# A recurrent kernel's opening: how its first inputs are read and turned

## The chip, the cores and the metric

The kernel runs on one core of one Trainium2 chip. The metric is the device time of one execution in microseconds (us); lower is better. The engines are called as the profile calls them: PE (TensorE, matrix products), DVE (VectorE), ACT (ScalarE), POOL (GpSimd) and SP (SyncE, which here only starts DMA transfers). Each engine works through its own instructions in program order and waits on semaphores for the others.

## What is computed

A gated recurrent unit over 128 steps for a batch of 64, with input and state 512 wide; every fourth step the state is sent through one more layer. The output is the input plus the states.

```python
def step(h, inp):
    x_t, prop = inp
    comb = jnp.concatenate([x_t, h], axis=-1)
    z = jax.nn.sigmoid(comb @ Wz + bz)
    r = jax.nn.sigmoid(comb @ Wr + br)
    comb2 = jnp.concatenate([x_t, r * h], axis=-1)
    h_cand = jnp.tanh(comb2 @ Wh + bh)
    h_new = (1.0 - z) * h + z * h_cand
    h_next = jnp.where(prop, jnp.tanh(h_new @ Wp + bp), h_new)
    return (h_next, h_new)
_, ys = jax.lax.scan(step, h0, (xs, do_prop))
return jnp.transpose(ys, (1, 0, 2))
...
x = x + _L0_cond_ref(x, cond_1024, ...)
```

x is 64 x 128 x 512 (batch, step, width), h0 64 x 512, the three gate matrices 1024 x 512 (the upper half, called wx in the kernel, meets x; the lower half, wh, meets h), Wp 512 x 512, all float32.

## The kernel before

The batch is split in two halves of 32 (h) and the width in four quarters of 128 (q); a step of x or h lies in on-chip memory as 128 partitions (quarter, batch row) by 2 x 128. For a product the state or the input must stand turned, width on the partitions. h is turned by DVE's transpose (L963); x by the same instruction at L547, in `join(t)`, which writes `xT`.

The part of the gates that comes from x doesn't depend on the state. It is made for groups of four steps at a time and kept in `cp`. For steps 0 to 3, `plain(t)` makes it with ordinary products of `xT` and `wx` (L392 is the line of the helper that emits every matmul), and DVE adds the biases on the way out of PSUM (L759). From group 1 (steps 4 to 7) on, `batch` makes it with a two-level fast scheme (Strassen's): seven products of seven, for which sums of pieces of `wx` (`tt`, `tf`, `tw`, L592, most on POOL, some on DVE, once at the start) and sums of pieces of `xT` (`s12r`, `o12`, `o34`, ..., L624 to L661, on POOL, in every group) must stand ready. The results are folded together by POOL (L848) and placed into `cp` by ACT and by DMA. From step 2 on the recurrent products use a one-level scheme of the same kind (`gates_seven`).

All operations are first collected in a plan: each has an engine, what it reads and writes, and a cost. The order in which they are then emitted comes from a table, `ORDER`, a compressed list of positions, found by a search beforehand; it fixes the order on each engine. PE's products of x fill the time in which the recurrence waits for other engines.

In the opening (L481 to L535) the transfers are these. SP starts two quarters of x of step 0, then wx: rows 0 and 1 of the gates R and Z in four pieces of 256 KB (`load_wx(..., True)`), the rest of R, Z and H in sixteen pieces of 128 KB, one per quarter of the partitions and pair of rows; then wh of R, Z and H, Wp, its bias, and later steps of x. ACT starts the other two quarters of step 0, the four of step 1 and three bias rows. POOL starts x of steps 2 and 3 (eight pieces), h0 (four) and x of steps 4 to 7 (eight). Two one-element copies on POOL, `held` (L456), stand ahead of these: the first waits until step 0 of x has landed, the second, ahead of x 4 to 7, until the last quarter of the Z weights has. Steps 0 to 7 of x stay in `xj`, where the output is later formed in place.

PE begins with 42 idle products of zeros (L900). The rows of x are read in pieces of 512 bytes (one quarter of one batch row).

Of the kernel before, what the change touches and what calls it, by code (L numbers as in the profile page):

```python
# [13 lines left out]
ALU = mybir.AluOpType  # L14
# [146 lines left out]
c-n2-2VhoNoha~oZtuO9@B0#x5E#lhGdj*VIyy}qM@L<Ku5aAkQFql{x4G`FK6Tv?S}3805_$<G0Rn^`I)oZ}C!qugW#|wXAhh>CH(?z2z5C;T%Kw~u^W`h|  # L161
o|}XXi1^@78$v()^oCIK3-tZ}u@T?<-e^R?_HE)X{(``Je}}Lviy(}5KKQ_Z?TrsV{P2Gfo!i@Q3xe><*My(`MBra~>B}#DzHk1sp&mV6e%2(u`qf^&-X@5*
;9uV7KKJ?jmkVEd>7|$7eDke$--X6Ezxkc_zw*X6UwZf5Z@l~NTf~>sUEX-*3s7ddbg9kj(xs4a;DE_zk{(HQo<+>eo0$iX$;7q$qGi6cI&W;A^ZfG#y?gg|
9mjE<L3!BFylw>1)i3HkJ<o&rg)ctJJ<1gp7UtXk{c#TK;^p_sCtMf4l6^VXA-J9U2$+|09sYS>-aqH%`R25|>p9Cx<ny_o|2&RuyE!K}<(hJF9EV|K1=fLF
hyAINyp~)`?re_G3BvO%{1vw6zIiCOEjK=IOYRxpPrp}-c<Zfq-d>p-o3}F84`O9*EySjrq9~#$YMP0R#ks{fRaJ>sKmW?-YIE3%Ts07H<U~=a%3+E!JI77W
O^5WH90~%QLmW3bH!U}@Q;&%`W<rkRxbZo1T+VVBTi1u@M(6DK1!QP_bAxhasS%yEK~X(=49xY-mFETkT6xYb&2{Jpf%9^4Nv<S^o@V>xo@PsPUG3tcBElAL
WyQPM{G!4a^Yd?IF-^Ocy_Th~W-;8v^@Z$}PoT@$%h{}w%Mm0K!jpPBdm?)(J1Xx~wnK<ovOxgvw}@!VPRWJGvd6N`kl&X*+Ua=q9Ar*++ME6Eq3oe-6!Ckq
!MBfQljOa|EXFrxzp*uowq<vuwt?-bZ7H4?d465?ZQFL%W}jJ;HBG`@optN8^;y<55ls>rT9K9IW!WX!8i+bjpIr(iZZFR+gQ!crydb*(rp(VGeI6W!Ig%Bs
v#MH^eWp4)FsIJV5;L+hvIJ4|-1O}9?5ymR>~kzDNrF%bQ;NoB$7ZKyi7DCfFfa$c+3{J4;U!6$l^vIz219tlsO%U}2?SaYIIdf_ZbP%fvwgEeQr4*Kz!W_w
%Muht<rl&BD5GiZnfA<+%)QLx)bQ+s4E8wFA6li^Tn^q__h7;RI7lWhuQc19d6>DAxev10?5)hLOdE7Rh65;>jG`14Mg^BLmon&b23Hq5UCM+PGZ+3$p)7al  # L170
# [1145 lines left out]
```

## Time and profile before

| | |
|---|---|
| median of three runs | 1226.2 us (1226.2, 1226.74, 1223.36) |
| the profiled execution | 1223.71 us |
| its span, first to last instruction | 1221.9 us |
| mean granted clock of PE | 0.998 |
| PE busy from 0 to 2 us, and from 60 to 80 us | 0.80 us, 19.85 us |
| HBM read, written | 24.84 MB, 16.78 MB |

The span is what the profile shows; the execution's own time is 1.8 us more. A row of a timeline gives the start, the time, the engine, the line, the operation, what it writes and reads, how many such instructions are merged, and in brackets the idle time of the engine before it with what ended it. A busy time is a share of one stretch: PE's is near full in almost all of them.

### The profile page before, as it was taken

To read this page: it belongs to the slowest core of one execution; us is meant where nothing else is said; L and a number is where in the kernel's file an instruction comes from. 1 tells how busy PE (TensorE), PEld (TensorE's weight loads), DVE (VectorE), ACT (ScalarE), POOL (GpSimd) and SP (SyncE) were. 2 spreads that over 40 slices of the span, in tenths; PEclk is the share of its full clock that TensorE was granted. 3 is DMA by queue.
4 is the path that set the end of the run, shared out by engine and by line. 5 is a ranking of instruction groups with operands and counts; after the bars stand their busy time and mean duration, and the time that the engine had idled before them with its cause. 6 is when DMAs were issued, how large, how long until landed. Compare 5 with 4: busy or idle time off the path is not lost.

```text
span 1221.9 us, 85156 instructions
## 1 busy us (share of the span) xinstructions
PE 1203.6 (99%) x37418; PEld 1151.8 (94%) x37418; DVE 866.6 (71%) x2833; ACT 778.6 (64%) x2309; POOL 960.1 (79%) x1510
## 2 busy tenths in 40 slices
PE   8799999999999999999999999999999999999997
PEld 5689999999999999999999999999999999999997
DVE  3967776677777777777776767777676777767775
ACT  1366666666666666666666666666666666666663
POOL 7998778787877887787887878876888878778852
PEclk9999999999999999999999999999999999999999
DMA  8212122122221222122212222211222212221122
GB/s 227 68 44 58 50 68 58 50 53 53 58 57 52 58 54 53 44 53 59 55 45 59 53 57 61 53 49 51 56 58 53 51 47 59 56 59 46 43 54 58
DMA packets 92018, 71.48 MB, mean 58 GB/s; under 512 B 7484, under 2 KB 87484, under 8 KB 91647
## 3 DMA queue, kind: packets, MB, share of 16 engines
q1 hardware_dynamic: 90328, 64.84, 20.5%
q8 instruction: 294, 4.82, 1.6%
q0 software_dynamic: 640, 0.92, 0.3%
q14 instruction: 78, 0.63, 0.2%
q10 hardware_dynamic: 678, 0.27, 0.1%
HBM read 24.84 MB, written 16.78 MB: 34 GB/s over the span
## 4 chain that ended last, share of the span: by engine, by line
PE 94%; POOL 3%; DMA 1%; issue 0%; DVE 0%; ACT 0%; SPq 0%; ACTq 0%; POOLq 0%; DVEq 0%
PE ps_e L392 16%; PE ps_r L392 15%; PE ps_b L392 13%; PE ps_y L392 12%; PE ps_x L392 12%; PE ps_q L392 11%; PE ps_z L392 9%; PE ps_a L392 6%; POOL tt L592 2%; DMA wx<-in_L_cond_Wh_dram 0%; DMA wx<-in_L_cond_Wz_dram 0%; DMA wh<-in_L_cond_Wr_dram 0%; POOL tf L592 0%; DMA xj<-in_x_dram 0%; POOL tw L592 0%
## 5 line engine op out<-in xcount | busy, mean ns | idle before, releaser
L392 PE MATMUL ps_z<-wh,sa 128*32 128x128 f32 x3904 | 168.7, 273 | 0.4 <-issue 0.4
L1058 POOL TENSOR_TENSOR sa<-hT 128x64 f32<-128x64 f32 x244 | 77.1, 322 | 111.6 <-DVE hT L963 80.1
L848 POOL TENSOR_TENSOR st<-mb,mb 128x768 f32<-128x768 f32 x77 | 141.1, 1833 | 10.1 <-ACT cp L872 4.3
L392 PE MATMUL ps_r<-wh,rhT 128*32 128x128 f32 x4096 | 144.8, 273 | 0.7 <-DVE rhT L963 0.7
L392 PE MATMUL ps_e<-wh,rhT 128*32 128x128 f32 x4096 | 144.5, 273 | 0.1
L963 DVE STREAM_TRANSPOSE hT<-h 128x128 f32<-128x128 f32 x318 | 97.4, 309 | 54.8 <-ACT h L1010 42.6
L392 PEld LDWEIGHTS ps_z<-wh,sa 128*32 128x32 f32 x3904 | 131.9, 110 | 3.5 <-issue 1.0
L848 POOL TENSOR_TENSOR mb<-mb,mb 128x768 f32<-128x768 f32 x62 | 113.8, 1835 | 19.7 <-ACT mb L815 14.3
L392 PEld LDWEIGHTS ps_r<-wh,rhT 128*32 128x32 f32 x4096 | 125.5, 110 | 3.1 <-DVE rhT L963 1.3
L1152 POOL TENSOR_TENSOR xj<-xj,h 128x256 f32<-128x256 f32 x127 | 93.2, 735 | 44.7 <-DVE h L1135 44.3
L872 ACT COPY cp<-st 64x384 f32<-64x384 f32 x248 | 125.0, 508 | 5.2 <-POOL st L848 1.0
L392 PEld LDWEIGHTS ps_e<-wh,rhT 128*32 128x32 f32 x4096 | 124.6, 110 | 1.9 <-DVE rhT L963 0.4
L1066 DVE TENSOR_TENSOR ps_z<-ps_z,keep 128x128 f32<-128x128 f32 x244 | 72.2, 296 | 41.9 <-PE ps_z L392 33.1
L1006 ACT COPY ps_r<-cp 128x128 f32<-128x128 f32 x256 | 69.2, 270 | 47.1 <-DVE h L1135 29.1
L392 PE MATMUL ps_y<-tw,s 128*32 128x192 f32 x1488 | 98.1, 328 | 0.1
L848 POOL TENSOR_TENSOR st<-mb 128x768 f32<-128x768 f32 x47 | 86.2, 1834 | 12.2 <-ACT cp L872 5.0
L392 PE MATMUL ps_e<-wh,hT 128*32 128x128 f32 x2144 | 90.6, 273 | 1.5 <-ACT ps_e L1006 0.7
L547 DVE STREAM_TRANSPOSE xT<-xj 128x256 f32<-128x256 f32 x128 | 82.6, 657 | 10.8 <-DMA xj<-in_x_dram 10.7
L1058 POOL TENSOR_TENSOR sa<-hT,sa 128x64 f32<-128x64 f32 x244 | 78.5, 322 | 12.5
L392 PE MATMUL ps_r<-wt,hT 128*32 128x128 f32 x1952 | 84.9, 273 | 0.0
L392 PE MATMUL ps_b<-wh,hT 128*32 128x128 f32 x1952 | 84.4, 273 | 0.0
L392 PE MATMUL ps_b<-wt,sa 128*32 128x128 f32 x1952 | 84.3, 273 | 0.0
(179 smaller groups left out, 3617.8 us busy)
## 6 DMA issues: line engine op xcount, KB each, us to landing
cp<-st SPq DMA_DIRECT2D x248, 96.0 KB
out_dram<-xj SPq DMA_DIRECT2D x254, 64.0 KB
xj<-in_x_dram SPq DMA_DIRECT2D x240, 64.0 KB
wx<-in_L_cond_Wh_dram SPq DMA_DIRECT2D x8, 128.0 KB
wh<-in_L_cond_Wr_dram SPq DMA_DIRECT2D x8, 128.0 KB
wh<-in_L_cond_Wz_dram SPq DMA_DIRECT2D x8, 128.0 KB
wh<-in_L_cond_Wh_dram SPq DMA_DIRECT2D x8, 128.0 KB
wp<-in_L_cond_Wp_dram SPq DMA_DIRECT2D x8, 128.0 KB
```

What stands on the lines that cost most here:

```text
L392: nc.tensor.matmul(dst, lhsT=lhsT, rhs=rhs, start=start, stop=True, skip_group_check=True)
L547: lambda: nc.vector.transpose(out=xT_(g)[:, i].rearrange("p c (a h b) -> p h (c a) b", a=S, h=S), in_=xj(t).rearrange("p h (e k) -> p h k ...
L592: fn = {"+": lambda: eng.tensor_add(dst, a, b), "-": lambda: eng.tensor_sub(dst, a, b)}[op]
L848: el("pool", 768, lambda: nc.gpsimd.tensor_add(dst, a, b), reads, writes, rank=FOLD)
L872: el("act", 384, lambda h=h, own=own: nc.scalar.copy(cp_(2 * g + a)[own, nb, h].rearrange("p b g u -> p (b g u)"), st_(n)[own, h].rearrang ...
L963: add("dve", 0.23, lambda: nc.vector.transpose(out=dst, in_=src), reads, writes, land=0.08, main=True)
L1006: el("act", n, lambda: nc.scalar.copy(dst, src), reads, writes, "+" + bank, main=True)
L1058: tensor(lambda: nc.gpsimd.tensor_sub(sa[:, n], a, b), reads, [("sa", t, n)], n=64, engine="pool")
L1066: tensor(lambda: nc.vector.tensor_add(dst, a, b), reads, writes, used_)
L1152: el("pool", 256, lambda: nc.gpsimd.tensor_add(x_out, x_out, h_(new_)), [("h", new_, 0), ("h", new_, 1)] + xk_, xk_)
```

## The change

Steps 0 to 3 of x are read as whole rows: one transfer of 64 rows of 2 KB per step (`load_flat`) into memory that the fast scheme uses only later (`spare`, two of the three `mb` buffers). They are turned by PE: `turn_x` multiplies a piece of the rows with a 64 x 64 unit matrix (`square`, made by POOL with a memset and an affine_select), 16 products per step, into the PSUM banks q and y, and DVE copies the result to `xT`. SP starts step 0, ACT steps 1 to 3.

All of wx is loaded in twelve pieces of 256 KB (gate and row), R and Z first, H last. h0 and x of steps 4 to 7 are started by SP instead of POOL, h0 behind wx, x 4 to 7 behind wh of R; x of steps 0 to 3 is loaded a second time, in the layout that the output needs, behind all of wh. The `held` copies are gone. 16 idle products stand where 42 stood. The order table is replaced as a whole (its encoded text is left out here).

A switch `ONE` is added by which products of group 1 could skip the inner level of the fast scheme (`flat=`, `rows_of`, `one`, `twos`); it is empty, so none does, and its hunks are left out.

```diff
@@ -317,6 +335,8 @@
     U2 = J // 2
     U4 = J // 4
     R, Z, H_ = range(3)
+    IDLES = 16
+    ONE = ()
     assert V * NQ == P and D == H and J == P and T % 8 == 0
 
     RINGS = {
@@ -351,13 +371,15 @@
     bias_row = wt.rearrange("p a k n -> p (a k n)")[0:1, : 3 * H].rearrange("p (i n) -> p i n", i=3)
     ones = wt.rearrange("p a k n -> p (a k n)")[0:1, 3 * H : 3 * H + V]
     dummy = new("dummy", [1, 1])
-    held = new("held", [P, 2])
+    square = wt.rearrange("p a k n -> p (a k n)")[0:B, 3 * H + B : 3 * H + 2 * B]
 
     steps_in = new("xj", [P, RINGS["xj"], S, J])
     xT_ = ring("xT", [P, Q4, C, P])
     cp_ = ring("cp", [P, C, S, 2, 3, U2])
     mb_ = ring("mb", [P, 2, 2, S, 3, U2])
     st_ = ring("st", [P, S, 2, 3, U2])
+    spare = [mb_(n).rearrange("p m b h g u -> p (m b h g u)")[:B] for n in (-1, -2)]
+    flat = lambda t: spare[t // 3][:, t % 3 * H : (t % 3 + 1) * H]
     xj = lambda t: steps_in[:, t % RINGS["xj"]]
     bias_x = steps_in[:, -2:].rearrange("p t h j -> p (t h j)")[:, : 3 * J].rearrange("p (c i u) -> p c i u", c=C, i=3)
     c5_ = ring("c5", [P, 2, S, 3 * U4])
@@ -418,13 +440,8 @@
     def queue(engine):
         return {"sp": nc.sync, "actq": nc.scalar, "poolq": nc.gpsimd}[engine]
 
-    def load_step(t, q, engine):
-        load(
-            engine,
-            lambda: queue(engine).dma_start(
-                out=xj(t)[part(q)], in_=x[:, t, ts(q, J)].rearrange("(h b) j -> b h j", h=S)),
-            [("xj", t, h, q) for h in range(S)], size=32.0, cost=0.4,
-        )
+    def load_flat(t, engine):
+        load(engine, lambda: queue(engine).dma_start(out=flat(t), in_=x[:, t, :]), [("xn", t)], size=128.0)
 
     def rows(ap, t, h):
         return ap[ts(h, V), t, :].rearrange("b (q j) -> q b j", q=NQ)
@@ -436,25 +453,9 @@
             if t < 3 * Q4:
                 plan.behind.append((late, op.index))
 
-    def load_wx(i, k, wide=False):
-
+    def load_wx(i, k):
         w = gates_in[i][:D].rearrange("(p k) n -> p k n", k=K)
-        if wide:
-            load("sp", lambda: nc.sync.dma_start(out=wx[:, k, i, :], in_=w[:, k]),
-                 [("wx", 0, i, k)], size=256.0, cost=0.43)
-            return
-        for q in range(NQ):
-            load(
-                "sp",
-                lambda q=q: nc.sync.dma_start(out=wx[part(q), k : k + 2, i, :], in_=w[part(q), k : k + 2]),
-                [("wx", 0, i, k + n, q) for n in range(2)], size=128.0, cost=0.43,
-            )
-        for n in range(2):
-            plan.whole(("wx", 0, i, k + n), [("wx", 0, i, k + n, q) for q in range(NQ)])
-
-    def hold(n, src, reads):
-        op = add("pool", 0.1, lambda: nc.gpsimd.tensor_copy(held[P - V : P, n : n + 1], src), reads, [("held", n)])
-        heads.setdefault("poolq", []).append(op.index)
+        load("sp", lambda: nc.sync.dma_start(out=wx[:, k, i, :], in_=w[:, k]), [("wx", 0, i, k)], size=256.0, cost=0.43)
 
     def load_wh(dst, w, keys, over=(), ks=K):
 
@@ -479,49 +480,56 @@
         )
 
     add("dve", 0.3, lambda: nc.vector.memset(zeros, 0.0), (), [("zeros", 0)])
+    add("pool", 0.16, lambda: nc.gpsimd.memset(square, 0.0), (), [("square", 0)])
+    add("pool", 0.25, lambda: nc.gpsimd.affine_select(
+        out=square, in_=square, compare_op=ALU.not_equal, fill=1.0, base=0,
+        pattern=[[-1, B]], channel_multiplier=1), [("square", 0)], [("square", 0)])
     add("pool", 0.2, lambda: nc.gpsimd.memset(ones, 1.0), (), [("ones", 0)])
-    for q in range(NQ):
-        load_step(0, q, ("sp", "actq")[q % 2])
-    load_wx(R, 0, True)
-    for q in range(NQ):
-        load_step(1, q, "actq")
-    for i, k in ((Z, 0), (R, 1), (Z, 1)):
-        load_wx(i, k, True)
+    begin = len(plan.ops)
+    load_flat(0, "sp")
+    load_flat(1, "actq")
+    load_wx(R, 0)
+    load_flat(2, "actq")
+    load_wx(Z, 0)
+    load_flat(3, "actq")
+    load_wx(R, 1)
+    load_wx(Z, 1)
     for i in range(3):
         load_bias(i)
-    opening = list(range(2, len(plan.ops)))
+    opening = list(range(begin, len(plan.ops)))
     plan.behind += list(zip(opening, opening[1:]))
-    for i, k in ((R, 2), (Z, 2), (H_, 0), (H_, 2)):
+    for i, k in ((R, 2), (Z, 2), (R, 3), (Z, 3), (H_, 0), (H_, 1), (H_, 2), (H_, 3)):
         load_wx(i, k)
     add(
         "act", 1.5, lambda: nc.scalar.activation(dummy, ones[:, 0:1], AF.Sigmoid),
         [("ones", 0)], [("dummy", 0), ("row_free", 0)],
     )
-    hold(0, xj(0)[P - V : P, 0, 0:1], [("xj", 0, 0, 3)])
-    for t in (2, 3):
-        for q in range(NQ):
-            load_step(t, q, "poolq")
     for q in range(NQ):
         load(
-            "poolq",
-            lambda q=q: nc.gpsimd.dma_start(
+            "sp",
+            lambda q=q: nc.sync.dma_start(
                 out=h_(0)[part(q)], in_=h0[:, ts(q, J)].rearrange("(h b) j -> b h j", h=S)
             ),
             [("h", 0, h, q) for h in range(S)], size=32.0,
         )
     for h in range(S):
         plan.whole(("h", 0, h), [("h", 0, h, q) for q in range(NQ)])
-    hold(1, wx[P - V : P, 3, Z, 0:1], [("wx", 0, Z, 3, 3)])
-    for h in range(S):
-        for q in range(NQ):
-            load(
-                "poolq",
-                lambda h=h, q=q: nc.gpsimd.dma_start(
-                    out=steps_in[part(q), Q4 : 2 * Q4, h, :], in_=x[ts(h, V), Q4 : 2 * Q4, ts(q, J)]),
-                [("xj", t, h, q) for t in range(Q4, 2 * Q4)], size=64.0,
-            )
-    for i in range(3):
+
+    def load_four(g):
+        for h in range(S):
+            for q in range(NQ):
+                load(
+                    "sp",
+                    lambda h=h, q=q: nc.sync.dma_start(
+                        out=steps_in[part(q), g * Q4 : (g + 1) * Q4, h, :], in_=x[ts(h, V), g * Q4 : (g + 1) * Q4, ts(q, J)]),
+                    [("xj", t, h, q) for t in range(g * Q4, (g + 1) * Q4)], size=64.0,
+                )
+
+    load_wh(wh[0], gates_in[0][D:], ("wh", 0, 0))
+    load_four(1)
+    for i in (1, 2):
         load_wh(wh[i], gates_in[i][D:], ("wh", 0, i))
+    load_four(0)
     load_wh(wp, Wp, ("wp", 0))
     for q in range(NQ):
         load("sp", lambda q=q: nc.sync.dma_start(
@@ -552,7 +560,7 @@
             [("xT", g, i)], land=0.08,
         )
         turns.append(turned.index)
-        if 0 < t < 2 * Q4:
+        if Q4 < t < 2 * Q4:
             plan.behind.append(tuple(turns[-2:]))
 
     def outer(kb, nb, ka):
...
@@ -901,9 +932,29 @@
                 bank.rearrange("p a n -> p (a n)")[part(i % NQ)], lhsT=zeros[:, :V], rhs=zeros,
                 start=True, stop=True), reads, writes or [("bits", 0)], rank=1e6)
 
-    idle(42)
+    idle(IDLES)
+    turn_keys = [take("q"), take("y")]
+
+    def turn_x(t):
+        bank = "qy"[t % 2]
+        ps = scratch[bank].rearrange("p a n -> p (a n)")[:, t // 2 * C * P : (t // 2 + 1) * C * P]
+
+        def unit():
+            for k in range(K):
+                for q in range(NQ):
+                    mm(ps[part(q), ts(k, B)], flat(t)[:, q * P + k : (q + 1) * P : K], square, True)
+
+        n = -1 - t // 3
+        own = [("turned", t)]
+        first = [turn_keys[t % 2]]
+        old = [("mb", n, m, b, a) for m in range(2) for b in range(2) for a in range(2)]
+        add("pe", 0.46, unit, [("xn", t), ("square", 0)] + ([] if t < 2 else first),
+            own + (first if t < 2 else []) + old + [("row_free", 0)], "+" + bank)
+        el("dve", 256, lambda: nc.vector.tensor_copy(xT_(0)[:, t].rearrange("p c n -> p (c n)"), ps),
+           own + first, [("xT", 0, t)], bank)
+
     for t in range(Q4):
-        join(t)
+        turn_x(t)
     spread_key = take("y")
     spread_ps = scratch["y"][:, 0:3]
 
```

More of the change, by code (lines that the diff above doesn't have):

```diff
@@ L796, in blocks, with one @@
             return [("mb", n, m, b, a) for m in range(2)]
+        def one(bank, m, left, right, reads, first):
+            def unit():
+                for h in range(S):
+                    for c in range(2):
+                        mm(ps[bank][part(2 * h + c), m].rearrange("p d (g u) -> p d g u", g=3),
+                           left[:, ts(h, V)], right[:, c::2], first)
+            add("pe", 0.327, unit, reads + ([] if first else [key[bank]]), [key[bank]], "+" + bank)
         def product(bank, j, start):
@@ L802, in product @@
                 right, rk = factor(i, j)
[L804 to L810 removed]
+                one(bank, m, left, right, lk + rk, first)
                 plan.due += long / count
```

318 lines of the change are left out of this document (175 added, 143 removed).

## The prediction

> **What bounds the kernel now.** The page first: one engine, TensorE, fills the span.
>
> ```profile
> span 1221.9 us, 85156 instructions
> PE 1203.6 (99%) x37418; PEld 1151.8 (94%) x37418; DVE 866.6 (71%) x2833; ACT 778.6 (64%) x2309; POOL 960.1 (79%) x1510
> ```
>
> The 99% is an average, so I read the busy time by stretches next. A row has the stretch, its length, busy time and instructions of PE, PEld, DVE, ACT and POOL, the granted clock, the DMA share and GB/s.
>
> ```profile
> 30.00:40.00 10.00, 9.06 (x244) 6.39 (x232) 9.93 (x14) 3.09 (x10) 9.92 (x10) 1.00 0.70 185
> 40.00:50.00 10.00, 7.52 (x211) 6.06 (x215) 9.38 (x19) 4.54 (x14) 10.00 (x12) 1.00 0.12 33
> 50.00:60.00 10.00, 6.72 (x216) 5.76 (x205) 9.79 (x17) 3.75 (x11) 9.84 (x9) 1.00 0.01 2
> 200.00:1210.00 1010.00, 1008.45 (x31692) 979.45 (x31685) 721.50 (x2427) 669.84 (x1989) 789.01 (x1254) 1.00 0.21 54
> ```
>
> From 200 to 1210 us PE rests 1010 - 1008.45 = 1.55 us: little can be won there. From 30 to 60 us it rests 30 - 9.06 - 7.52 - 6.72 = 6.7 us while POOL and DVE are full. Whatever brings forward the moment from which PE rests no more brings the end forward by as much. That moment is found in the chain of waits, cut to the first 66 us:
>
> ```profile
> 16.38 3.57 DMA wh<-in_L_cond_Wr_dram
> 19.94 0.54 POOL xj L519
> ...
> 20.61 1.00 POOL tt L592
> ...
> 59.49 0.70 POOL o L661
> ...
> 60.77 1.43 PE ps_r L392 x32
> ```
>
> Loads until about 20 us, then POOL's sums (of weights at L592, and of x) from 20.61 to 60.19 us, 39.6 us, then PE for good. So the start of POOL's sums is what counts, and POOL's timeline comes next:
>
> ```profile
> 15.91 0.18 POOL L456 COPY held<-wx 32x1 f32<-32x1 f32 x1 [4.71 <-DMA wx<-in_L_cond_Wz_dram]
> 16.14 4.34 POOL L519 DMA_DIRECT2D xj<-in_x_dram  x8
> 20.61 0.99 POOL L592 TENSOR_TENSOR tt<-wx 128x384 f32<-128x384 f32 x1
> 23.74 1.71 POOL L592 TENSOR_TENSOR tt<-wx 128x384 f32<-128x384 f32 x1
> ```
>
> The chain names DMAs ahead of 19.94 us, but the first sum starts 0.13 us after POOL has issued the last load of x 4 to 7 (16.14 + 4.34 = 20.48). POOL's own issuing, held back by the copy that waits for the last quarter of the Z weights, set the start.
>
> **The change part by part.** *Issuing leaves POOL.* Eight loads of x 2 and 3, four of h0, eight of x 4 to 7 and both "held" copies go. POOL gains two small operations on a 64x64 unit matrix, in the first microseconds, where it has nothing else. The first sum (inner(1)) reads rows 0 and 1 of wx of all three gates, so it can start when the second H piece has landed. How soon is that? By bytes:
>
> ```profile
> 0.00:8.00 8.00, 6.80 (x106) 3.59 (x106) 1.59 (x3) 1.49 (x2) 4.25 (x14) 1.00 0.61 183
> 8.00:12.00 4.00, 2.83 (x66) 1.93 (x64) 0.65 (x1) 0.00 (x0) 3.00 (x6) 1.00 0.99 259
> 12.00:14.00 2.00, 0.28 (x12) 0.01 (x2) 0.19 (x1) 0.00 (x0) 0.00 (x0) 1.00 0.98 249
> 14.00:16.00 2.00, 1.50 (x44) 1.29 (x48) 0.73 (x3) 0.00 (x0) 0.09 (x1) 1.00 0.95 231
> 16.00:24.00 8.00, 8.00 (x191) 5.37 (x184) 2.03 (x7) 0.75 (x2) 7.66 (x13) 1.00 0.94 240
> 24.00:28.00 4.00, 4.00 (x104) 2.35 (x100) 3.96 (x4) 1.13 (x3) 4.00 (x3) 1.00 1.08 242
> 28.00:30.00 2.00, 2.00 (x72) 1.82 (x68) 2.00 (x3) 0.00 (x0) 2.00 (x4) 1.00 1.07 239
> ```
>
> Summed, 1464 + 1036 + 498 = 2998 KB have moved by 14 us. Ahead of the end of the second H piece stand four steps of x (131 KB each) and ten pieces of wx (262 KB each), 3146 KB: moved at 14 + 148 / 231 = 14.6 us. A landing comes later than that: the Z quarter that released the held copy at 15.91 us had 2752 KB ahead of its end (x 0 to 3, h0, eight pieces), moved at 13.0 us, so it lagged by 2.9 us. The start thus lies between 14.6 us (no lag) and 17.5 us (all of it). I take 16.5 us, nearer to the row with the lag: **4.1 us earlier** than 20.61, with ends of 6.0 and 3.1.
>
> That lag is weighed against a page. The Trainium skill, "DMA: Bandwidth & Descriptors", section "Latency and other measured facts", says that DMA engines 7 and 15 tend to be slower and guesses that the descriptor rings of DMAs issued from GpSimd cause it. By it the lag would go with POOL's issues and the gain would be the end of 6.0 us; the views of this run don't show the engines apart, so I don't take it.
>
> *Does the rest keep up, 4.1 us earlier?* POOL's 39.6 us of sums are the same, so PE must be done sooner with what stood before 60 us. Its rests are 1.17 + 1.72 + 0.50 = 3.4 us from 8 to 16 us (rows above) and the 6.7 us, 10.1 in all. The early ones are waits for weights and for steps 2 and 3 of x, whose turning on DVE starts late:
>
> ```profile
> 10.50 0.65 DVE L547 STREAM_TRANSPOSE xT<-xj 128x256 f32<-128x256 f32 x1 [3.54 <-DMA xj<-in_x_dram]
> 13.81 0.63 DVE L547 STREAM_TRANSPOSE xT<-xj 128x256 f32<-128x256 f32 x1 [2.66 <-DMA xj<-in_x_dram]
> 50.70 0.41 DVE L759 TENSOR_TENSOR cp<-ps_b,xj 128x256 f32<-128x256 f32 x1
> ```
>
> The change loads all four steps with the first weights and adds 64 turning matmuls. The trace has none of 64 rows and 64 columns; 16 of 128 columns follow each other in 0.44 us (65.08 to 65.52 in the last fence of this part), so the four steps cost between nothing (PE waits for loads then) and 1.8 us. I charge 1.8. Of 10.1 us, 1.8 and 4.1 leave 4.2 us of rest: PE doesn't become the bound, and 10.1 - 1.8 = 8.3 us is the most that an earlier POOL can bring. The 26 idle matmuls less cost nothing; they filled PE's wait. DVE loses four transposes of 0.65 us and gains four copies out of PSUM, at 0.41 us by its addition of that size, where it waits anyway.
>
> *SP's queue.* x 4 to 7 move behind wh's R part:
>
> ```profile
> 35.55 0.45 POOL L626 TENSOR_TENSOR s12r<-xT 128x128 f32<-128x128 f32 x1
> 38.18 1.06 PE L392 MATMUL ps_z<-wh,hT 128*32 128x128 f32 x32
> 36.83 2.75 SPq L527 DMA_DIRECT2D bias_p<-in_L_cond_bp_dram  x4
> ```
>
> Ahead of their end stand 5.37 MB, moved at 24.0 us, landed by 26.9 with the lag. POOL first needs them, after four transposes of 0.65 us, at 35.55 - 4.1 = 31.4 us: 1.9 us of cover. Ahead of the end of wh's Z part stand 6.42 MB as before, moved at 28.3 us, landed by 31.2; PE's first use moves from 38.18 to 34.1 us: 2.9 us of cover. The second load of x 0 to 3 and all behind it come when the DMA is near rest (0.12 from 40 us on). These cost nothing unless SP issues slowly (rivals). The x loads on ACT's queue delay only the biases and ACT, which is idle.
>
> *The clock.* After its longest rest PE ran slowly:
>
> ```profile
> 59.55 0.53 PE L392 MATMUL ps_q<-tw,o 128*32 128x192 f32 x8 [3.28 <-POOL o L659]
> 60.24 0.53 PE L392 MATMUL ps_q<-wx,o 128*32 128x192 f32 x8 [0.15 <-POOL o L661]
> 60.59 1.61 PE L392 MATMUL ps_r<-wh,rhT 128*32 128x128 f32 x32
> 61.95 1.53 PE L392 MATMUL ps_x<-tt,o 128*32 128x192 f32 x16
> 63.23 1.39 PE L392 MATMUL ps_y<-tw,s 128*32 128x192 f32 x16
> 64.43 0.83 PE L392 MATMUL ps_q<-tt,s 128*32 128x192 f32 x16
> 65.08 0.62 PE L392 MATMUL ps_b<-wh,hT 128*32 128x128 f32 x16
> 65.52 0.51 PE L392 MATMUL ps_a<-tw,o 128*32 128x192 f32 x8
> 62.00:64.00 2.00, 2.00 (x32) 1.39 (x28) 0.78 (x3) 0.95 (x4) 1.92 (x3) 0.50 0.00 0
> ```
>
> From 60.59 to 64.43 us three groups take 3.84 us. At the pace of the rows behind them (0.65 us from 64.43 to 65.08 for 16 of 192 columns, twice 0.44 for 32 of 128) they take 2.2. The granted clock of 0.50 cost 1.7 us. With 4.2 us of rest instead of 10.1, one of 3.3 us is less likely, but the order inside the opening decides. Ends 0 and 1.7; I take the middle, **0.8 us**.
>
> *The searched order.* After 60 us it can win about the 1.55 us above and has no lower bound; I take nothing.
>
> **The sum.** The profiled execution took 1223.7 us, 1.8 around its span. 1223.7 - 4.1 - 0.8 = 1218.8 us. The median of the three runs, 1226.2, stands 2.5 us above it; runs like that would give 1221.3, inside my range.
>
> **The rivals.**
>
> *More.* If the lag vanishes (6.0 us) and the slow clock with it (1.7), the time is 1216.0 us. If PE becomes the bound, 1223.7 - 8.3 - 1.7 = 1213.7. For it: no early load is issued from POOL any more. Against: the lag is seen, its cause isn't.
>
> *Another wait takes its place.* Two forms. First, a POOL sum takes 0.99 us at 20.61, while DVE rests, and 1.71 at 23.74, when DVE sums weights too. If DVE's sums now start together with POOL's, the first three pay 0.7 us each: 2.1 of the 4.1 us go. The Trainium skill, "GPSIMD Engine Reference", section "1. Specifications", says the two engines share their SBUF interfaces and contend when DVE reads two SBUF inputs; by that rule the price is paid wherever both sum, and the 0.99 and 1.71 us agree. Second, SP: at 2.75 / 4 = 0.69 us per issue the eight loads of x 4 to 7 take 5.5 us, where their 0.52 MB need 2.1, and wh's Z part lands at 34.6 us, half a microsecond after its use, with x 4 to 7 past their cover. Either way about 2 us are left: 1221.7 us, between 1220 and 1224. That the start hardly moves (H landing near 20 us) belongs here, at 1223.
>
> *Slower: the searched order stalls the steady stretch.* In that loop POOL is busy 789 of 1010 us with sums that PE's products wait for, and PE rests so little only because the old order has each sum ready. If the new one has them late by 0.04 us in each of the 124 steps, the 4.9 us are eaten; at 0.1 us the time is 1218.8 + 12.4 = 1231. For it: the whole table is replaced. Against: POOL has 22% in hand.
>
> **How the numbers follow.** Forecast 0.45 (1217 to 1221), more 0.22 (1213 to 1217), another wait 0.21 (1220 to 1224), slower 0.12 (1225 to 1235). A measurement of this kernel can tell about 0.3%, 3.7 us, from no change, so faster means below 1220.0 us. Of the forecast 0.34 lies there, 0.22 and 0.03 of the next two: 0.59. Within 0.3%: 0.11, 0.18 and 0.01 of the slower case, 0.30. Slower: 0.11. The range, 1213 to 1226, leaves out most of the slower case and allows for the 2.5 us between runs.
>
> **What would show it.** POOL's first sum (tt, 128x384) near 16.5 us with no DMA issue before it; hardly a rest of PE from 8 to 16 us; PE's last rest before steady work ending near 56 us, with clock 0.50 behind it or not; PE's rest from 200 to 1210 us near 1.5 us. I am wrong if that sum starts at 19 us or later, if PE rests more after 100 us, or if the last such rest still ends near 60 us although the first sum came early.

## The result and the profile after

The changed kernel took 1218.75 us (median of 7 runs, 1214.81 to 1220.01), the kernel before beside it 1224.59 us (7 runs, 1222.24 to 1226.74). The ratio is 0.995, with a 95% interval of 0.9933 to 0.9966: 5.8 us less. The profiled execution also took 1218.75 us.

The page of the changed kernel has the same picture as before, 5.0 us shorter:

```profile
span 1216.9 us, 85315 instructions
PE 1202.9 (99%) x37520; PEld 1157.4 (95%) x37520; DVE 864.1 (71%) x2833; ACT 777.8 (64%) x2309; POOL 949.1 (78%) x1490
```

PE's busy time hardly changes, so what went is rest. The stretches of the changed kernel show where (columns as in the prediction):

```profile
0.00:8.00 8.00, 5.12 (x139) 3.73 (x139) 1.17 (x4) 1.49 (x2) 0.84 (x8) 1.00 0.76 221
8.00:12.00 4.00, 3.57 (x56) 2.56 (x60) 0.71 (x2) 0.00 (x0) 0.00 (x0) 1.00 0.85 280
12.00:14.00 2.00, 2.00 (x60) 1.50 (x56) 0.00 (x0) 0.00 (x0) 0.00 (x0) 1.00 0.83 253
30.00:40.00 10.00, 9.07 (x262) 7.35 (x257) 9.64 (x20) 3.88 (x11) 9.92 (x14) 1.00 0.62 174
40.00:50.00 10.00, 8.82 (x272) 8.18 (x263) 6.25 (x15) 4.08 (x15) 8.45 (x12) 1.00 0.46 135
50.00:60.00 10.00, 9.80 (x285) 8.72 (x288) 9.70 (x23) 5.83 (x17) 9.69 (x12) 1.00 0.11 29
62.00:64.00 2.00, 2.00 (x72) 1.00 0.40 106
200.00:1210.00 1010.00, 1007.31 (x31692) 983.25 (x31684) 720.82 (x2424) 667.33 (x1984) 784.88 (x1246) 1.00 0.21 53
```

From 40 to 60 us PE rested 5.76 us and now rests 1.38; from 62 to 64 us (a row with PE alone) it has the full clock, where it had half. From 200 to 1210 us it rests 2.69 us instead of 1.55. The timeline of the changed kernel shows the new start, and a wait that wasn't there before:

```profile
4.25 1.09 PE L414 MATMUL ps_q<-wt,mb 64*32 64x64 f32 x32 [1.59 <-DMA mb<-in_x_dram]
8.43 4.29 PE L414 MATMUL ps_z<-wx,xT 128*32 128x128 f32 x64 [0.54 <-DVE xT L953]
...
14.78 1.78 POOL L600 TENSOR_TENSOR tf<-wx 128x384 f32<-128x384 f32 x1 [13.34 <-DMA h<-in_cond_dram]
16.53 1.71 POOL L600 TENSOR_TENSOR tt<-wx 128x384 f32<-128x384 f32 x1
18.31 1.60 POOL L600 TENSOR_TENSOR tt<-tt,wx 128x384 f32<-128x384 f32 x1
...
43.31 2.60 SPq L535 DMA_DIRECT2D bias_p<-in_L_cond_bp_dram  x4
49.11 0.27 ACT L1057 COPY ps_r<-bias_p 128x128 f32<-128x128 f32 x1 [2.15 <-DMA bias_p<-in_L_cond_bp_dram]
49.41 0.29 DVE L1075 TENSOR_TENSOR rh<-ps_r,h 128x128 f32<-128x128 f32 x1 [2.70 <-ACT ps_r L1057]
50.20 1.08 PE L414 MATMUL ps_r<-wh,rhT 128*32 128x128 f32 x32 [1.38 <-DVE rhT L1014]
```

POOL starts its sums 5.8 us earlier. (The bracket names the load of h0, which that sum doesn't read; h0 stands behind the last piece of wx on SP's queue, and such names are inferred.) x of steps 0 to 3 is turned by 7.9 us, and DVE's copies to `xT` are done by 8.7. At 49 us ACT waits for `bias_p`, the bias of the layer that follows every fourth step: SP issues it at 43.31 us instead of 36.83, behind h0, x 4 to 7, and x 0 to 3 a second time, twenty loads that it didn't have before (wx takes eight loads fewer).

The end of one execution is a blunt gauge: it moves by some us between runs. So I also use a **landmark** in the trace: the start of the first candidate product of the 17th step (`ps_e<-wh,rhT`, the 513th of 4096). It is the same instruction in every kernel here, read off one execution of each. In the kernel before it is this row (the view ends at 204 us, so it lists 20 of the 32 products),

```profile
203.53 0.73 PE L392 MATMUL ps_e<-wh,rhT 128*32 128x128 f32 x20
```

and in the changed kernel this one:

```profile
198.53 1.06 PE L414 MATMUL ps_e<-wh,rhT 128*32 128x128 f32 x32
```

5.0 us earlier, just as the end of the span. At the 65th step the two are 5.7 us apart, at the 127th 5.5: little is won or lost behind the opening.

### The profile page after: what moved, and what is told of

Read it like the earlier page. It is cut to its first block, busy times and chain, and to the rows that moved or that the text cites. A ratio compares the mean times of both kernels' runs of the same rounds, so it can differ in the third digit from the quotient of the medians.

```text
span 1216.9 us, 85315 instructions
## 1 busy us (share of the span) xinstructions
PE 1202.9 (99%) x37520; PEld 1157.4 (95%) x37520; DVE 864.1 (71%) x2833; ACT 777.8 (64%) x2309; POOL 949.1 (78%) x1490
## 4 chain that ended last, share of the span: by engine, by line
PE 91%; SPq 3%; POOL 2%; DMA 2%; issue 1%; DVE 1%; ACT 0%; ACTq 0%; DVEq 0%
PE ps_e L414 15%; PE ps_r L414 15%; PE ps_b L414 13%; PE ps_x L414 11%; PE ps_q L414 11%; PE ps_y L414 11%; PE ps_z L414 9%; PE ps_a L414 6%; SPq L468 1%; SPq L523 1%; DMA wx<-in_L_cond_Wh_dram 0%; DMA cp<-st 0%; DMA wx<-in_L_cond_Wr_dram 0%; POOL st L879 0%; POOL tt L600 0%
## 5 line engine op out<-in xcount | busy, mean ns | idle before, releaser
L414 PE MATMUL ps_z<-wh,sa 128*32 128x128 f32 x3904 | 164.8, 273 | 0.0
L414 PEld LDWEIGHTS ps_z<-wh,sa 128*32 128x32 f32 x3904 | 128.0, 110 | 3.6 <-issue 0.6
L414 PE MATMUL ps_y<-tw,s 128*32 128x192 f32 x1488 | 94.5, 326 | 0.0
L1014 DVE STREAM_TRANSPOSE rhT<-rh 128x128 f32<-128x128 f32 x256 | 78.5, 309 | 6.9
L414 PE MATMUL ps_r<-wt,hT 128*32 128x128 f32 x1952 | 82.3, 273 | 0.0
```

The costliest lines, as they stand in the source:

```text
L414: nc.tensor.matmul(dst, lhsT=lhsT, rhs=rhs, start=start, stop=True, skip_group_check=True)
L1014: add("dve", 0.23, lambda: nc.vector.transpose(out=dst, in_=src), reads, writes, land=0.08, main=True)
```

## The experiments

All of them in one table. The ratio is to the kernel before, run beside each; "first sum" is the start of POOL's first sum of weights. "Old" and "new" is the order table. The medians of the kernel before lie between 1223.9 and 1225.9 us from one set of runs to the next, so times of different rows can be told apart only to some 2 us; the ratios are the safer comparison.

| run | order | median us (runs) | ratio, 95% interval | first sum us | landmark us |
|---|---|---|---|---|---|
| before | old | 1224.59 (7) | | 20.61 | 203.5 |
| changed | new | 1218.75 (7) | 0.995 (0.9933 to 0.9966) | 14.78 | 198.5 |
| e1_issue_only | old | 1225.35 (12) | 0.9994 (0.9979 to 1.0008) | 18.65 | 201.5 |
| e6_x_only | old | 1226.13 (12) | 1.0 (0.9987 to 1.0014) | 20.43 | 202.7 |
| e11_o_early | old | 1224.35 (12) | 1.0002 (0.9989 to 1.0014) | 21.09 | 203.2 |
| e12_loads_only | old | 1225.08 (12) | 1.0009 (0.9998 to 1.002) | 18.71 | 202.2 |
| e10_order_alone | new | 1221.48 (12) | 0.9978 (0.9966 to 0.9989) | 18.59 | 199.1 |
| e9_wx_pieces | new | 1219.54 (5) | 0.9949 (0.9931 to 0.9967) | 17.16 | 200.1 |
| e2_issue_back | new | 1219.65 (5) | 0.9944 (0.9928 to 0.9959) | 20.77 | 198.5 |
| e7_order_only | new | 1217.96 (6) | 0.9941 (0.9922 to 0.9959) | 14.03 | 196.7 |
| e4_idle_31_more | new | 1221.05 (10) | 0.9956 (0.9939 to 0.9972) | 14.67 | 197.1 |
| e8_bias_idle | new | 1218.88 (7) | 0.9954 (0.9936 to 0.9973) | 15.04 | 197.0 |
| e3_bias_early | new | 1216.37 (4) | 0.992 (0.9904 to 0.9936) | 14.37 | 196.4 |

### The issuing, taken out of one kernel and put back in the other

In the kernel before, h0 and x of steps 4 to 7 go to SP; nothing else changes:

```diff
-            "poolq",
-            lambda q=q: nc.gpsimd.dma_start(
+            "sp",
+            lambda q=q: nc.sync.dma_start(
                 out=h_(0)[part(q)],
...
```

> The kernel before with one part of the change: h0 and x 4 to 7 are issued by SP, and the second held copy is gone; x 0 to 3 are still turned by DVE, order table as before. Theory A (the end follows the start of POOL's sums): the first sum starts at 17 to 18 us instead of 20.6, when the H weights have landed, and the time falls by 2.5 to 3.5 us, ratio to before about 0.9975. Theory B (what counts is PE's own time in the opening: late x of steps 2 and 3, rests before 16 us): the sums start earlier just the same, but the time falls by less than 1 us.

Measured: the first sum came 1.96 us earlier and PE's last long rest ended at 57.89 us instead of 59.55. The landmark moved by 2.0 us too. The time didn't move beyond its interval, which reaches from 2.6 us less to 1.0 more: by its trace this run is Theory A with a smaller step, by its time Theory B, and the time can't tell 2.0 us from none.

In the changed kernel the same loads go back to POOL, ahead of its sums and behind two held copies:

```diff
+        if op.name == ("t5", 0, 1):
+            for n, (i, k) in enumerate(((R, 2), (Z, 3))):
+                nc.gpsimd.tensor_copy(held[P - V : P, n : n + 1], wx[P - V : P, k, i, 0:1])
+                for o in early[n]:
+                    o.emit()
```

> The changed kernel with that part undone: POOL issues h0 and x 4 to 7 again, ahead of its sums, behind two one-element copies that wait for rows 2 of R and 3 of Z of wx. The first sum then starts near 17.3 us instead of 14.8. Theory A: the time rises by 2 to 3 us against the changed kernel, to about 1221. Theory B: it rises by less than 1 us.

Measured: the first sum starts at 20.77 us, later than expected and where it was before the change, and the gain is there all the same: landmark 198.5, time 0.9 us above the changed kernel and well inside its interval. By the letter that is Theory B. But the comparison isn't clean: with twelve loads fewer ahead of it on SP's queue, `bias_p` is there in time. Against the next run, made beside the same runs of the kernel before, which doesn't wait for `bias_p` either, a start 6.4 us later costs 2.2 us at the landmark, a third, and 3.3 us of time (1219.65 against 1216.37, and the slowest run of the one is faster than the fastest of the other), about half. So in the new order POOL's start sets a part of the end, not all of it.

### The new wait

In the changed kernel ACT issues the load of `bias_p`, behind the three bias rows:

```diff
-        load("sp", lambda q=q: nc.sync.dma_start(
+        load("sp", lambda q=q: nc.scalar.dma_start(
             out=bias_p[part(q)],
...
```

> The changed kernel with the four loads of bias_p issued by ACT behind the bias rows instead of by SP at 43 us. In the changed kernel ACT waits 2.15 us for this load at 49 us, and behind it DVE's rh waits 2.7 us, POOL 1.4 and PE 1.4. If this new wait is on the path that sets the end, the time falls by 1.4 to 2 us against the changed kernel (to about 1217); if POOL's sums up to 60 us set it anyway, it stays within 0.5 us.

The timeline of this run has the copy without a wait:

```profile
47.67 0.27 ACT L1057 COPY ps_r<-bias_p 128x128 f32<-128x128 f32 x1
```

and its stretches have PE full, as the rows of PE alone show:

```profile
40.00:50.00 10.00, 10.00 (x330) 1.00 0.55 151
50.00:60.00 10.00, 10.00 (x296) 1.00 0.08 22
```

Against the changed kernel the landmark moves forward by 2.2 us and the time by 2.4, to 1216.37 us: the fastest kernel here, faster than both. The change had lost about that much to the length of SP's queue.

### Idle products

31 more at the start, 47 in all (the text below says 42, as before), in the changed kernel:

```diff
+    MORE = 31
...
-            add("pe", 0.107, lambda bank=bank, i=i: nc.tensor.matmul(
+            add("pe", 0.107, lambda bank=bank, i=i: [nc.tensor.matmul(
...
+                start=True, stop=True) for m in range(1 if i else 1 + MORE)], reads, writes or [("bits", 0)], rank=1e6)
```

> The changed kernel with 31 more products of zeros at its start, so that 42 stand there as before. In the changed kernel PE turns and multiplies slowly until about 11.5 us (the first 64 products with wx take 4.1 us, where 64 records take 1.75 later). If the idle products ripen the clock as before (full from about 6.3 us) and PE's time counts: the turning starts 1.5 us later, but PE gains 2 to 3 us by 12 us, and the time falls by 0.5 to 2 us. If the arrival of wx sets the pace until 12 us, it stays the same within 0.5 us. If the late turning counts, it rises by 1 to 1.5 us.

The timeline of this run shows the first products of wx at full pace, 48 in 1.94 us, where the changed kernel needs 4.29 us for 64:

```profile
8.27 1.94 PE L415 MATMUL ps_z<-wx,xT 128*32 128x128 f32 x48 [0.55 <-DVE xT L954]
10.80 1.06 PE L415 MATMUL ps_z<-wx,xT 128*32 128x256 f32 x14 [0.59 <-DMA wx<-in_L_cond_Wz_dram]
...
17.77 3.23 PE L415 MATMUL ps_x<-wx,xT 128*32 128x128 f32 x62 [1.38 <-issue]
```

But PE then rests 0.59 us for a piece of wx and 1.38 us for which the profile names nothing, and `ps_y<-wt`, at 20.01 us in the changed kernel, starts at 20.93. The landmark is 1.4 us earlier, but not from there, and the time isn't lower. The same with 19 more, on top of the early `bias_p`:

> The changed kernel with the load of bias_p issued by ScalarE behind the bias rows (1216.4 us by itself) and 19 more idle products at the start, 30 in all. If the slow clock at the start costs time (full clock near 8 us instead of 11.5 us, so 64 products of ps_z of 4.1 us become about 2.1 us), the time falls by 0.5 to 1.5 us. If the arrival of wx sets the pace until 30 us, PE rests that much more behind the turned products and the time is the same within 0.7 us.

Neither came: the landmark is 0.6 us later than with the early `bias_p` alone, the time 2.5 us higher. Idle products bring nothing that these times can show.

### The x path, alone and left out

In the kernel before, x of steps 0 to 3 is read as whole rows and turned by PE, everything else stays:

```diff
+            lambda: None if q else (nc.scalar if t else nc.sync).dma_start(out=flat(t), in_=x[:, t, :]),
...
+            for k in range(K):
+                for q in range(NQ):
+                    mm(ps[part(q), ts(k, B)], flat(t)[:, q * P + k : (q + 1) * P : K], square, True)
```

> The kernel before with one part of the change alone: x of steps 0 to 3 comes as whole rows on SyncE's and ScalarE's queues and is turned by TensorE with the unit matrix, and is read a second time behind bias_p for the second layer. h0 and x of steps 4 to 7 stay on GpSimd's queue behind the held copies, wx keeps its pieces, and the order is the old one. Theory X (the early x carries the gain, since PE then has work where it rested 8 to 16 us): TensorE starts its first products of layer 0 near 8.5 us instead of near 16, and the time falls by 3 to 4.5 us below the kernel before. Theory O (the newly searched order carries it, since PE's rests between 40 and 66 us go from 6 to 1.5 us): the rests of 40 to 66 us stay, and the time is that of before within 1.2 us. Theory S (the start of GpSimd's sums sets the end, as in the prediction): the first sum stays at 20 to 21 us, and the time is that of before within 1 us.

By its time this is Theory O's outcome, and Theory S's as well, since the first sum stays at 20.43 us: 1226.13 us. PE's rest from 0 to 40 us falls from 5.52 to 4.15 us; with 128 turning products more PE is busy 0.8 us longer up to the landmark, which comes 0.9 us earlier. In the changed kernel the opposite: x 0 to 3 in pieces of 512 bytes and turned by DVE (step 3 takes the place of step 0, and 47 idle products stand ahead, not 42).

```diff
+            for q in range(NQ):
+                by = ((nc.sync, nc.scalar)[q % 2], nc.scalar, nc.gpsimd, nc.gpsimd)[n]
+                by.dma_start(out=xj(t)[part(q)], in_=x[:, t, ts(q, J)].rearrange("(h b) j -> b h j", h=S))
```

> The changed kernel with its new order, its wx pieces and SyncE's loads of h0 and x of steps 4 to 7, but x of steps 0 to 3 read in pieces of 512 bytes and turned by VectorE, as in the kernel before; there are no turning products, no second load, and 42 idle products as before. Theory X: TensorE rests again until near 16 us and the time goes back up by 2 to 4 us, to 1221 to 1223 us. Theory O: the order absorbs the late x, and the time stays within 1 us of the changed kernel. With both parts needed (the early work is of use only if the order has no rest behind it): both this run and the run with the x part alone lie less than 2 us below the kernel before.

1217.96 us: Theory O again. This run has no second load of x, so `bias_p` is in time; against the run with the early `bias_p` (landmark 196.4) it lies at 196.7. Reading whole rows and turning them on PE changes nothing that can be measured, in either order.

### The pieces of wx

```diff
+            if k < 2 and i < 2:
+                nc.sync.dma_start(out=wx[:, k, i, :], in_=w[:, k])
+            elif k % 2 == 0:
+                for q in range(NQ):
+                    nc.sync.dma_start(out=wx[part(q), k : k + 2, i, :], in_=w[part(q), k : k + 2])
```

> The changed kernel with wx in the pieces of before: rows 0 and 1 of R and Z as whole pieces of 256 KB, the others as quarter pieces that hold a pair of rows. If the twelve pieces matter, the wx of the third gate lands later or earlier by more than 1 us and the time moves by more than 1 us; if only the bytes count, landing times move by less than 1 us and the time is within 1 us of the changed kernel.

Between the two: the first sum comes 2.4 us later and the landmark 1.6, the time stays within 1 us.

### Order and loads, each by itself

The new order with every load as before the change (the parts of the runs e2, e7 and e9 together, so step 3 of x comes first and 47 idle products stand ahead):

> The newly searched order with every load as in the kernel before: x of steps 0 to 3 in pieces of 512 bytes and turned by VectorE, wx in its old pieces, h0 and x of steps 4 to 7 on GpSimd's queue ahead of its sums, 42 idle products. As a landmark serves the 17th step of the recurrence, whose first candidate product starts at 203.5 us in the kernel before, 198.5 in the changed one and 196.7 in the one with the order and SyncE's loads. Theory O (the order carries the gain by itself): the landmark lies at 197 to 199 us, GpSimd's first sum stays near 20 us, PE rests less than 2 us between 40 and 66 us, and the time is 1217.5 to 1220 us. Theory L (the order needs the loads that let GpSimd start near 14 us): PE rests 3 us or more between 30 and 66 us, the landmark lies at 201 us or later, and the time is 1221.5 us or more.

The old order with every load as in the changed kernel; its diff is that of e6, that of e1 (here both held copies go), and:

```diff
-                lambda q=q: nc.sync.dma_start(out=wx[part(q), k : k + 2, i, :], in_=w[part(q), k : k + 2]),
+                lambda q=q: None if q > 1 else nc.sync.dma_start(out=wx[:, k + q, i, :], in_=w[:, k + q]),
```

> The counterpart of the run with the order alone: the old order with every load as in the changed kernel. x of steps 0 to 3 comes as whole rows and is turned by TensorE, wx comes in twelve whole pieces, h0 and x of steps 4 to 7 are on SyncE's queue, and GpSimd has no held copies and issues nothing ahead of its sums. Theory A (the prediction's: GpSimd's start sets the end as long as PE rests for GpSimd's work, and in the old order it does): the first sum starts at 14.5 to 16.5 us instead of 20.6, PE's last long rest ends 4 to 6 us earlier than 59.55 us, the first candidate product of the 17th step starts at 197.5 to 200 us instead of 203.5, and the time falls by 3.5 to 6 us. Theory N (an earlier start is lost within GpSimd's queue, to the doubled time of sums beside VectorE's and to a new wait for ScalarE's st as with SyncE's issuing alone): the last long rest ends after 57.5 us, the landmark lies at 201 us or later, and the time falls by less than 2 us.

These two decide. PE's busy time of the order alone, in two stretches:

```profile
0.00:40.00 40.00, 32.71 (x723) 0.96 0.87 217
40.00:66.00 26.00, 26.00 (x784) 1.00 0.13 34
```

The kernel before:

```profile
0.00:40.00 40.00, 34.48 (x794) 1.00 0.84 217
40.00:66.00 26.00, 20.08 (x532) 0.93 0.05 14
```

The loads alone:

```profile
0.00:40.00 40.00, 36.75 (x914) 1.00 0.74 210
40.00:66.00 26.00, 22.23 (x592) 0.93 0.17 45
```

With the new order PE doesn't rest at all from 40 to 66 us, although it has done 1.8 us less by 40 us and POOL's first sum starts at 18.59. That brings the landmark forward by 4.4 us and the time by 2.9. Theory O holds for the rests and the landmark; the time is near the lower bound of Theory L, so the loads have a part in it as well. With the loads alone PE still rests 3.8 us there, and the time is not lower: Theory N.

What each part does shows in a count. Up to the landmark PE does the same products in all these kernels, but for the idle and the turning ones: the numbers in the traces differ by just these. The landmark is then PE's busy time plus its rests:

| run | products up to the landmark | rest to 40 us | rest from 40 us to the landmark | busy us |
|---|---|---|---|---|
| before | 5626 | 5.52 | 6.02 | 191.99 |
| loads alone | 5754 (128 turning more) | 3.25 | 3.77 | 195.18 |
| order alone | 5631 (5 idle more) | 7.29 | 0.41 | 191.40 |
| changed | 5728 (128 turning more, 26 idle fewer) | 4.25 | 2.11 | 192.17 |
| early `bias_p` | 5728 (the same) | 3.76 | 0.28 | 192.32 |

The order takes away the rests behind 40 us, the loads some of those ahead of it, and both show in the last row, where nothing waits for `bias_p`. The loads alone cut PE's rests by 4.5 us, more than the order alone (3.8); but PE is busy 3.2 us longer with them, and 1.3 us are left at the landmark. So this run isn't a test of POOL's start by itself: it has the turning on PE as well, with all 42 idle products ahead of it.

POOL's sums do start earlier, and lose it again. That stands in POOL's timeline of that run:

```profile
18.71 1.00 POOL L606 TENSOR_TENSOR tt<-wx 128x384 f32<-128x384 f32 x1 [17.27 <-DMA wx<-in_L_cond_Wh_dram]
...
27.77 0.51 POOL L961 COPY bias_s<-st 128x192 f32<-128x192 f32 x1 [3.97 <-ACT st L954]
...
57.87 1.17 POOL L673 TENSOR_TENSOR o<-xT 128x256 f32<-128x256 f32 x1
```

The old order places h0 ahead of H on SP's queue, where its four issues take 1.9 us, and the first sum, which reads H, waits until 18.71 us, 3.9 us later than in the changed kernel. Then POOL stands 3.97 us before a bias sum that needs ACT's `st`. The 1.9 us won at the start are down to 0.46 at `o` (58.33 us before). In the new order more sums stand ahead of the bias sums, and POOL doesn't rest from 14.78 to 48.7 us.

### One place in POOL's queue

The kernel before, with only the two differences `o` ahead of the five sums that stood before them:

```diff
+        if op.name == ("tt", 0, 6, 2) and op.engine == "pool":
+            for o in moved:
+                o.emit()
```

> The kernel before with nothing changed but the place of two of GpSimd's operations: the differences o of L659 and L661, for which PE rested 3.28 us at 59.55 us, stand ahead of the five sums that ran from 51.60 to 58.33 us. Theory P (it is the place in GpSimd's queue that made PE rest): PE's rest near 59 us goes, and with it the drop of the clock; the landmark of the 17th step moves from 203.5 to 200 or 201 us, and the time falls by 2 to 4 us. Theory W (GpSimd's work as a whole is the bound there, and the same PE products then wait for sums that end 1.9 us later): PE rests 2 us or more for a sum in tt instead, the landmark moves by less than 1.5 us, and the time is that of before within 1.5 us.

```profile
62.85 0.86 PE L392 MATMUL ps_y<-tw,s 128*32 128x192 f32 x16 [2.94 <-POOL s L627]
```

That row is PE's timeline of this run: the rest of 3.28 us at 59.55 is gone and stands, 2.94 us long, four groups of products later, where PE now waits for a sum of x, `s`. The landmark moves by 0.3 us, and from 40 us to the landmark PE rests 5.8 us where it rested 6.0. (In this one execution the low clock stands elsewhere: 0.61 from 16 to 18 us and 0.53 from 18 to 20, behind a rest of 3.56 us.) So a place by itself wins nothing: in the old order PE asks for POOL's sums before POOL can have them all. The new order lets PE run ahead with the recurrence first: the first candidate product of the third step starts at 62.8 us instead of 71.7, 8.9 us earlier, and of this lead 5.0 us are left at the 17th.

## Why the prediction came out right, and which of its steps were wrong

1. **The number** was 1218.8 us; the median is 1218.75. The sum took 4.9 us off a profiled execution; its span became 5.0 us shorter. It was right by a sum of which the main term was put down to the wrong part; that it hit so closely is luck.
2. **POOL's start** was to move by 4.1 us and moved by 5.8. By bytes, with 221, 280 and 253 GB/s from 0, 8 and 12 us, the 3146 KB had moved at 13.0 us, not 14.6; the start came 1.8 us behind that, where 1.9 were taken. So the loads were mis-sized, not the lag.
3. **"Whatever brings forward the moment from which PE rests no more brings the end forward by as much."** This is the step that failed. The moment, the end of the last long rest, moved from 59.55 to 50.20 us (near 56 was forecast), 9.4 us, and the end by 5.0. What the end follows is the sum of PE's rests and its busy time up to the landmark: 5.2 us of rest went, and the busy time stayed within 0.2 us. That POOL's start carries the end holds at the landmark in the old order (1.96 us of start, 2.0 at the landmark), but only in part in the new one (6.4 us of start: 2.2 at the landmark and 3.3 of time, between two runs that don't wait for `bias_p`).
4. **"The searched order ... I take nothing."** It was the largest term: 4.4 us at the landmark and 2.9 in the time by itself, half of the 5.8, while all the loads without it brought 1.3 and nothing. The loads bring their half only together with the order. The step looked for the order's gain only behind 60 us, which it put at the 1.55 us of rest from 200 to 1210 us; its gain lies in the 5.9 us of rest from 40 to 66 us, which were counted as POOL's.
5. **The clock** behind the long rest was to bring 0.8 us. The rest and the 0.50 are gone. What it's worth by itself no run here separates: with the loads alone 0.50 stands from 44 to 46 us, with the order alone from 14 to 16.
6. **The turning** was charged 1.8 us and takes 3.4 (four times 0.85 us, from 4.25 to 7.9), at a slow pace. No time here shows that cost: alone in the old order PE's shorter rest (1.7 us up to the landmark) outweighs 0.8 us of longer work, and leaving it out of the changed kernel doesn't move the time. In the run of the loads alone it is part of the 3.2 us by which PE is busy longer.
7. **SP's queue** was costed at nothing, with a slow SP as a rival. PE and POOL wait for neither x 4 to 7 nor wh, as that step had it, and the eight issues of x 4 to 7 took 4.7 us where the rival had 5.5. But `bias_p`, which the step counted among "all behind it" though it shows the row of its issue, came late: 2.2 us at the landmark, 2.4 us in the time. A step that moves loads to a queue has to follow every load behind them.
8. **Two sums at once** came true as the rival had it: the first six sums took 1.60 to 1.78 us each instead of 1.0, with DVE's sums beside them from 14.73 us. In the run with the issuing put back the second to fourth take 1.00 to 1.02. The Trainium skill, "GPSIMD Engine Reference", section "1. Specifications", has the two engines share their SBUF interfaces; these rows agree. How much of that price reached the end isn't shown.
9. **The lag.** The Trainium skill, "DMA: Bandwidth & Descriptors", section "Latency and other measured facts", guesses that descriptor rings of GpSimd's DMAs slow two of the engines. With no early load issued from GpSimd the lag is 1.8 us by bytes instead of 2.9; it doesn't vanish, and no run here shows the engines apart.
10. **The steady stretch** rests 2.69 us, not 1.55. The slower rival, sums that come late in each step, didn't happen.

**What stays open.** Behind the landmark the kernels take between 1018.1 us (changed with early `bias_p`) and 1022.1 us (issuing alone; loads alone), in traces with the same clock. From 277 to 1210 us PE issues 29280 products in the kernel before and 29174 with the loads alone; it rests 1.55 us there in the one and 3.07 in the other, and no row shows where the other 2 us go. That is why the time follows the landmark only within about 2.5 us, and why the order alone and the loads alone (2.9 us less, 1.1 us more) don't add up to the 5.8.

## What to carry to other kernels

When a change replaces an order, the rests of the busiest engine are the order's to remove as much as the loads': price both against the same rests, and don't book them for one. Moving one late operation ahead in a full queue only moves the wait; the order that helped here asks for the work later and has something else to run meanwhile. To see what each part does, count the products up to one fixed instruction and set the engine's busy time and its rests up to there side by side. After moving loads to another queue, look at the last small one behind them, for here the late load of one bias cost 2.4 us.

## What the hardware showed beyond that

Products of 64 rows by 64 columns didn't bring PE to its full pace. In the changed kernel PE turns x from 4.25 to 7.9 us nearly without a rest, and the 64 products behind that still take 4.29 us; with 31 idle products of 512 columns more, 48 such products take 1.94 us and a turned step 0.54 to 0.73 us instead of 0.85. With 19 more and two rests of 0.49 and 0.30 us between the turned steps the next 64 products took 4.43 us again; there the granted clock says 0.50 from 10 to 12 us. In the changed kernel it says 1.00 from 8 to 12 us all the same, so that the slow pace there is the clock's is read from the pace alone.

Nor does it take one long rest to bring the clock down. With the loads alone 0.50 stands from 44 to 46 us behind four rests of 0.28 to 0.88 us between 38 and 43 us; in the run with the two differences moved, the clock stays at 1.00 from 40 to 66 us though PE rests 2.94 us at a stretch there.
